# The third last batch's routed row turned on TensorE, and the tiles behind the branch in a loop

## The chip, the core and the metric

The kernel runs on one core of a Trainium2 chip. The metric is the device time of one execution in microseconds (us). Five engines work side by side, each with its own instructions in a fixed order: TensorE (PE, with its weight loads PEld), VectorE (DVE), ScalarE (ACT), GpSimd (POOL) and SyncE (SP). SP issues most of the DMA transfers here, POOL those with computed addresses (scatters).

## The reference, cut to what matters

Two layers work on 16 batches of 256 tokens of width 256. Each layer is a cross attention and a feed-forward part, each added to x. The last part is a mixture of eight experts, and the change touches the way into it:

```
x = x + _L0_xattn_ref(ctx_1024, layernorm(x), ...)      # 8 heads of 128
x = x + _L0_ffn_ref(layernorm(x), ...)                  # weights depend on the batch's own tokens
x = x + _L1_xattn_ref(layernorm(x), ctx_1024, ctx_1024, ...)
x = x + _L1_ffn_ref(layernorm(x), ...):
    inh     = sigmoid(x @ Wr / temperature)             # 8 numbers per token
    weights = exp(-|inh - c| / 0.1) inside a zone, else the two nearest experts; normalized
    out     = sum over e of weights[e] * ((silu(x @ Wg[e]) * (x @ Wu[e])) @ Wd[e])
```

A token whose weight for an expert is zero need not be computed by it. The kernel sorts the tokens by expert and computes only those.

## The kernel before, in words

**Batches.** A batch goes through a front part (heads: `s0q`, `s0k`, `s1`, `s2`, `s3`) and a chain (`chain(b, A, behind)`): output projection `px`, feed-forward (`ph`, gelu, `pf`), second attention (`pv`, `pq`, `sc`, `po`), then the **row**: x normalized once more, with the token's number behind it. `row` is what the experts read, and it is also multiplied by the router's weights `Wr` (product `pl`, result `z`). `route(b, A, mine)` turns z into the eight weights (VectorE lines 737 to 787), counts the tokens of each expert (`pn`), works out slots, and scatters the rows into a DRAM tensor `slots_d` by POOL, 16 indirect DMAs per batch (line 811). Batches 0 to 11 are part 0 of the experts' work, 12 to 15 part 1.

**Turning.** Matmul needs its operand with the width on the partitions, so every normalized tile is transposed. There are two ways. `to_blocks` and `from_blocks` transpose 32 x 32 blocks on VectorE, write them to DRAM and read them back in the other order (a hop: one DMA out, four back, all from SP). `turned_tile` transposes 128 x 128 on TensorE into PSUM and copies the result out on ScalarE. A flag `hopped = b < B - 2` chooses for all four places in `chain`, so batches 14 and 15 are turned on TensorE and batches 0 to 13 hop. The place of the row is lines 616 to 629.

**Order.** The order on each engine is written by the program as it builds the kernel. `chain`, `route` and `experts` are generators; a `yield` gives a time (us of PE work, kept in `Clock.pe`) before which the job is not to be taken up again, and `gap()` lets waiting jobs put their next unit behind the heads' work. So a changed `yield` moves all that comes after it. `evict` copies a PSUM result out on ScalarE, or on VectorE while ScalarE is planned to be busy with a gelu (`Clock.act_free`). PSUM tiles of the tag "mm" turn through six buffers in the order in which they are asked for.

**Experts.** `experts(lists, ...)` starts with the last heads (batch 15, head 4 on) and runs beside the chains of batches 13 to 15. A group `G` is up to four tiles of 128 tokens of one expert, named by part, expert and first tile (group 0_4 of expert 0 is its tiles 4 to 6). Per group: `load` of rows from `slots_d`; turning (`turn_rows` on TensorE for the first two groups, a hop `send_rows` / `fetch_rows` for the others); gate `pg` and up `pu` for two halves; down `pd`; the weighted result `o` added into the output by a POOL DMA (line 1324).

**The branch.** Each expert has fixed room (`CAPS`). Tokens beyond it go through single tiles `U`, whose place and expert `plan()` works out on the chip (`Plan.starts`, `Plan.who`, `Plan.weigh`). Three such tiles are always computed among the groups (`AMONG = (2, 1)`); more would run behind `tc.If(some > 0)`, and if those do not suffice, `V` tiles in loops run over all slots.

Of the kernel before, what the change touches and what calls it, by code (L numbers as in the profile page):

```python
# [12 lines left out]
F32 = mybir.dt.float32  # L13
# [3 lines left out]
ALU = mybir.AluOpType  # L17
AX = mybir.AxisListType

P = 128  # L20
# [9 lines left out]
def xattn_ffn_kernel(  # L30
# [10 lines left out]
    nc = tc.nc  # L41
    B, S, D = x.shape
# [4 lines left out]
    E = Wg.shape[0]  # L47
# [39 lines left out]
    class Job:  # L87
# [3 lines left out]
        def __init__(self, units):  # L91
            self.units, self.ready, self.done = units, 0.0, False
# [12 lines left out]
    def apart(ins, group, others=()):  # L105

        for g in (group, *others):
            tc.declare_no_dep(
                ins.ins, group=g, reason="rows of one group go to different places"
            )  # L110
        tc.add_to_no_dep_group(group, ins.ins)
        nc.gpsimd.nop()
# [52 lines left out]
    UNITS = (6, 1)  # L165

    AMONG = (2, 1)
# [89 lines left out]
    ROW = D + E + 1  # L257
# [42 lines left out]
    def to_blocks(pool, src, C, tag, bufs, name, most=None):  # L300
        tb = pool.tile(
            [P, C * D], F32, tag=tag, bufs=bufs, name=name, padded_shape=[P, most or C * D]
        )
        tb = tb.rearrange("p (m d c s) -> p m d c s", m=QP, d=DC, c=C)
        for c in range(C):
            nc.vector.transpose(
                tb.rearrange("p m d c s -> p d m c s")[:, :, :, c, :],
                src[:, c, 0:D].rearrange("p (d m r) -> p d m r", d=DC, m=QP),
            )
        hop = dram.tile([P, QP, DC * C * QB], F32, tag=f"{tag}{C}", name=f"hop_{name}")  # L310
        nc.sync.dma_start(hop, tb.rearrange("p m d c s -> p m (d c s)"))
        return hop

    def from_blocks(dst, hop):
        from_ = hop.rearrange("(a r) m f -> m r a f", r=QB)
        for m in range(QP):
            nc.sync.dma_start(dst[ts(m, QB)].rearrange("r a d c s -> r a (d c s)"), from_[m])  # L317

    def in_order(t):

        return t.rearrange("p a d c s -> p d c a s")
# [25 lines left out]
    def chain(b, A, behind):  # L347
# [12 lines left out]
        hopped = b < B - 2  # L360
# [3 lines left out]
        def raw_tile(tag, name):  # L364
            return wk.tile([P, QP, DC, TC, QB], F32, tag=tag, name=name)

        def turned_tile(src, tag, name):
            t = wk.tile([P, DC, S], F32, tag=tag, bufs=1, name=name)
            nc.scalar.copy(t, transposed(src, f"{name}_p"))
            return t  # L370
# [24 lines left out]
        y = wk.tile([P, TC, D], F32, tag="y", name=f"yb_{b}")  # L395
# [22 lines left out]
        if hopped:  # L418
# [3 lines left out]
            yT, latents = in_order(yTb), yTb[:, 0, :, 0, :]  # L422
            there = Clock.pe + LANDED
        else:
            yield 2.2
            yT = latents = turned_tile(y, "yT", f"ybT_{b}")
# [99 lines left out]
        y = wk.tile([P, TC, D], F32, tag="y", name=f"yc_{b}")  # L526
# [86 lines left out]
        row = A.row[b] = wk.tile([P, TC, ROW], F32, tag="row", bufs=2, name=f"row_{b}")  # L613
        ln_apply(row[:, :, 0:D], x_b, mv, rs)
        nc.vector.tensor_copy(row[:, :, D + E], number[:, b * TC : (b + 1) * TC])
        if hopped:
            hop = to_blocks(wk, row, TC, "tbc", 2, f"yd_{b}_b")
            yield SENT
            raw = raw_tile("raw_c", f"ydT_{b}")
            from_blocks(raw, hop)  # L620
            yield LANDED
            ydT = wk.tile([P, DC, S], F32, tag="q1T", name=f"ydT_{b}")
            for d in range(DC):
                evict(ydT[:, d, :], in_order(raw)[:, d], None, None)
            yield 4.0
        else:
            yield 1.4
            ydT = turned_tile(row, "q1T", f"ydT_{b}")
            yield 1.6
# [201 lines left out]
    with ExitStack() as sh, ExitStack() as sa, ExitStack() as sf:  # L831
# [82 lines left out]
        def evict(out, src, bias, scale):  # L914

            if Clock.pe >= Clock.act_free:
                if bias is None:
                    nc.scalar.copy(out, src)  # L918
                else:
                    nc.scalar.activation(out, src, AF.Identity, bias=bias, scale=scale)  # L920
            elif bias is None:
                nc.vector.tensor_copy(out, src)
            else:
                nc.vector.tensor_scalar(out, src, scale, bias, ALU.mult, ALU.add)
# [259 lines left out]
        def add_chain(b, behind):  # L1184
            job = Job(chain(b, A, behind))
            A.tails[b] = Job(route(b, A, job))
            line.extend([job, A.tails[b]])
            return job
# [34 lines left out]
        class G:  # L1223
# [7 lines left out]
            def load(self):  # L1231
                self.rows = D_.front.tile(
                    [P, self.tiles, ROW], F32, tag="rows", name=f"rows_{self.name}",
                    padded_shape=[P, TG, ROW],
                )
                nc.sync.dma_start(
                    self.rows,
                    slots_d[self.part][self.first : self.first + self.tiles * P, :].rearrange(
                        "(t p) f -> p t f", p=P
                    ),  # L1240
                )
# [98 lines left out]
        def others(part):  # L1340

            k = 1 - part
            return [f"out_{k}_{e}" for e in range(E)] + [f"out_{k}_u{j}" for j in range(UNITS[k])]

        class U:


            def __init__(self, part, j):
                self.part, self.j = part, j
                self.u = sum(UNITS[:part]) + j  # L1350
                self.name = f"{part}_u{j}"

            def place(self):
                return nc.values_load(
                    Plan.starts[0:1, self.u : self.u + 1], engines=(mybir.EngineType.SP,),
                    min_val=0, max_val=E * NTOKS[self.part] - P,
                )

            def expert(self):
                return nc.values_load(  # L1360
                    Plan.who[0:1, self.u : self.u + 1], engines=(mybir.EngineType.PE,),
                    min_val=0, max_val=E - 1,
                )

            def weight(self, to):
                by = D_.more.tile([P, E], F32, tag="by_u", bufs=2, name=f"by_{self.name}")
                nc.vector.tensor_tensor(by, self.rows[:, D : D + E], Plan.weigh[:, self.u], ALU.mult)
                nc.vector.tensor_reduce(to, by, AX.X, ALU.add)

            def load(self):  # L1370
                tag = ("y", "yT")[self.u % 2]
                rows = wk.tile(
                    [P, ROW], F32, tag=tag, bufs=1, name=f"rows_{self.name}",
                    padded_shape=[P, DC * S],
                )
                self.rows = rows
                nc.sync.dma_start(rows, slots_d[self.part][bass.ds(self.place(), P), :])
# [37 lines left out]
            def down(self):  # L1415
# [13 lines left out]
                )  # L1429
                apart(ins, f"out_{self.name}", others(self.part))  # L1430

        class V(U):


            def __init__(self, part, e, t, j):
                self.part, self.u = part, j
                self.e, self.t = e, t
                self.name = f"{part}_v{j}"

# [107 lines left out]
        for n in range(NS + 2):  # L1547
            b, h = divmod(n, H)
# [55 lines left out]
        some = nc.values_load(beyond[0:1, 0:1], min_val=0, max_val=1)  # L1604
        all_slots = nc.values_load(beyond[0:1, 1:2], min_val=0, max_val=1)
        with tc.If(some > 0):
            for part in range(2):
                for j in range(AMONG[part], UNITS[part]):
                    u = U(part, j)
                    u.load()  # L1610
                    u.turn()
                    u.gates()
                    u.turn_h()
                    u.down()

            with tc.If(all_slots > 0):
                for part in range(2):
                    with tc.For_i(0, E) as e:
                        with tc.For_i(0, (NTOKS[part] - CAPS[part]) // P, 2) as t:
                            pair = [V(part, e, t + j, j) for j in range(2)]  # L1620
                            for v in pair:
                                v.load()
                            for v in pair:
                                v.turn()
                                v.gates()
                                v.turn_h()
                                v.down()
# [38 lines left out]
```

## Time and profile before

| what | value |
|---|---|
| median of three runs | 1810.41 us (1808.53 to 1811.94) |
| the profiled execution's own time | 1815.16 us |
| its span, first to last instruction | 1813.4 us |
| mean granted TensorE clock | 0.995 |
| HBM read and written | 161.91 MB and 161.48 MB, 178 GB/s over the span |
| last matmul group, last output DMA of POOL | 1799.8 us, 1802.6 us |

How to read it: times in the trace are microseconds from the span's start. The page gives busy shares of each engine, and the chain of work that ended last, followed back from the last instruction: an engine that is not on it costs nothing by being busy. The timeline prints start, duration, engine, line, what is written and read, and in brackets how long the engine was idle before it and which event ended that. Nearly all matmuls have line 80 (transposes line 84), the place of a helper; they are told apart by the names of their tiles. A row with xN is N instructions merged. The granted clock is the share of full speed that TensorE was given in a stretch.

The heads' part of the kernel ends at about 1460 us; from about 1430 to 1800 us the experts run.

### The profile page before, as it was taken

To read this page: it belongs to the slowest core of one execution; us is meant where nothing else is said; L and a number is where in the kernel's file an instruction comes from. 1 tells how busy PE (TensorE), PEld (TensorE's weight loads), DVE (VectorE), ACT (ScalarE), POOL (GpSimd) and SP (SyncE) were. 2 spreads that over 40 slices of the span, in tenths; PEclk is the share of its full clock that TensorE was granted. 3 is DMA by queue.
4 is the path that set the end of the run, shared out by engine and by line. 5 is a ranking of instruction groups with operands and counts; after the bars stand their busy time and mean duration, and the time that the engine had idled before them with its cause. 6 is when DMAs were issued, how large, how long until landed. Compare 5 with 4: busy or idle time off the path is not lost.

```text
span 1813.4 us, 22509 instructions
## 1 busy us (share of the span) xinstructions
PE 1780.6 (98%) x6508; PEld 1206.7 (67%) x6508; DVE 1196.6 (66%) x3332; ACT 586.0 (32%) x1306; POOL 830.9 (46%) x979
## 2 busy tenths in 40 slices
PE   8999999999999999999999999999999999999987
PEld 4566666666666666666666666666666677666655
DVE  4465676767676767676767676767666667675544
ACT  3433434343434343333333333333333311211100
POOL 2122224444435353535353535353534357776765
PEclk9999999999999999999999999999999999999999
DMA  6653546565655555555556555555545668899986
GB/s 215 184 185 117 174 139 190 167 189 168 187 169 188 168 184 172 184 172 178 173 181 174 180 177 177 179 178 175 181 156 157 197 161 216 227 234 235 200 168 112
DMA packets 264746, 325.01 MB, mean 179 GB/s; under 512 B 32893, under 2 KB 217385, under 8 KB 264617
## 3 DMA queue, kind: packets, MB, share of 16 engines
q1 hardware_dynamic: 235720, 273.67, 49.9%
q0 software_dynamic: 28848, 49.83, 11.7%
q8 instruction: 54, 0.88, 0.2%
q14 instruction: 76, 0.61, 0.1%
q10 hardware_dynamic: 48, 0.01, 0.0%
HBM read 161.91 MB, written 161.48 MB: 178 GB/s over the span
## 4 chain that ended last, share of the span: by engine, by line
PE 92%; DMA 2%; DVE 2%; SPq 1%; issue 1%; POOL 1%; ACT 0%; POOLq 0%; DVEq 0%; ACTq 0%
PE po L80 13%; PE sc L80 13%; PE pv L80 13%; PE pk L80 11%; PE pq L80 7%; PE px L80 6%; PE ph L80 6%; PE pf L80 6%; PE pg L80 5%; PE pu L80 5%; PE pd L80 5%; DMA yTd<-hop_rows_b 1%; PE pl L80 1%; SPq L317 1%; DMA pT<-hop 0%
## 5 line engine op out<-in xcount | busy, mean ns | idle before, releaser
L987 ACT ACTIVATE pr<-sc,nm 128x512 f32<-128x512 f32 x256 | 173.7, 683 | 479.7 <-DVE nm L981 418.4
L995 POOL TENSOR_SCALAR pr<-pr,ri 128x512 f32<-128x512 f32 x256 | 179.0, 709 | 322.7 <-DVE ri L994 317.8
L811 POOL DMA_INDIRECT slots_d<-row,at_slot x256 | 253.2, 989 | 70.4 <-issue 70.4
L80 PE MATMUL po<-pT,v 128*128 128x256 f32 x1024 | 242.3, 379 | 2.6 <-DVE W2T L1048 1.5
L80 PE MATMUL sc<-kT,qT 128*128 128x512 f32 x512 | 241.0, 593 | 1.5 <-ACT kT L920 1.5
L80 PE MATMUL pk<-kvT,Wk_sb 128*128 128x512 f32 x512 | 241.3, 594 | 0.0
L80 PEld LDWEIGHTS po<-pT,v 128*128 128x128 f32 x1024 | 193.8, 190 | 70.8 <-issue 38.1
L80 PE MATMUL pv<-Wv_sb,kvT 128*128 128x512 f32 x512 | 235.0, 592 | 0.0
L1033 DVE TENSOR_SCALAR outT<-po,cvec 128x256 f32<-128x256 f32 x128 | 61.2, 478 | 246.0 <-PE po L80 230.1
L1003 DVE STREAM_TRANSPOSE tb<-pr 128x512 f32<-128x512 f32 x256 | 165.9, 686 | 13.2 <-DMA hop<-tb 11.7
L80 PEld LDWEIGHTS pv<-Wv_sb,kvT 128*128 128x128 f32 x512 | 97.0, 190 | 108.2 <-issue 103.1
L981 DVE TENSOR_REDUCE nm<-sc 128x1 f32<-128x512 f32 x256 | 160.3, 663 | 2.0 <-PE sc L80 1.9
L80 PEld LDWEIGHTS sc<-kT,qT 128*128 128x128 f32 x512 | 96.9, 190 | 69.9 <-issue 61.2
L80 PEld LDWEIGHTS pk<-kvT,Wk_sb 128*128 128x128 f32 x512 | 97.7, 191 | 68.4 <-issue 61.6
L80 PE MATMUL pq<-kvT,Wq_sb 128*128 128x256 f32 x512 | 133.5, 383 | 0.0
L80 PEld LDWEIGHTS pq<-kvT,Wq_sb 128*128 128x128 f32 x512 | 96.7, 191 | 41.8 <-issue 28.2
L80 PE MATMUL px<-Wo_sb,outT 128*128 128x256 f32 x512 | 121.8, 381 | 0.0
L80 PE MATMUL ph<-ybT,W1e 128*128 128x256 f32 x512 | 121.0, 379 | 0.0
L1324 POOL DMA_INDIRECT out_dram<-o,at x65 | 102.3, 1574 | 36.3 <-issue 19.2
L452 POOL TENSOR_TENSOR W2e<-ev,od 128x256 f32<-128x256 f32 x120 | 78.5, 681 | 88.0 <-DMA ev<-ev_d 88.0
L918 ACT COPY v<-pv 128x512 f32<-128x512 f32 (+1 forms) x132 | 70.8, 536 | 148.1 <-PE pv L80 146.7
L80 PE MATMUL pf<-W2e,hT 128*128 128x256 f32 x512 | 118.0, 379 | 0.0
(259 smaller groups left out, 2695.4 us busy)
## 6 DMA issues: line engine op xcount, KB each, us to landing
hop<-tb SPq DMA_DIRECT2D x128, 512.0 KB
pT<-hop SPq DMA_DIRECT2D x512, 128.0 KB
ev<-ev_d SPq DMA_DIRECT2D x32, 512.0 KB
rows<-slots_d SPq DMA_DIRECT2D x14, 530.0 KB
hop_rows_b<-rows_b SPq DMA_DIRECT2D x13, 512.0 KB
yTd<-hop_rows_b SPq DMA_DIRECT2D x52, 128.0 KB
rows<-slots_d SPq DMA_DIRECT2D x15, 397.5 KB
hop_rows_b<-rows_b SPq DMA_DIRECT2D x14, 384.0 KB
```

What stands on the lines that cost most here:

```text
L80: nc.tensor.matmul(out, lhsT, rhs, **kw)
L317: nc.sync.dma_start(dst[ts(m, QB)].rearrange("r a d c s -> r a (d c s)"), from_[m])
L452: (nc.gpsimd if b < B - 1 else nc.vector).tensor_tensor(W2e[:, c, d, :].rearrange("p (i a) -> p i a", i=NI), evs[1][:, :, c * NA : (c + 1) ...
L811: ins = nc.gpsimd.indirect_dma_start(out=slots_d[part], out_offset=bass.IndirectOffsetOnAxis(ap=at_slot[:, c, e : e + 1], axis=0), in_=row ...
L918: nc.scalar.copy(out, src)
L981: nc.vector.tensor_reduce(nm, sc, AX.X, ALU.max, negate=True)
L987: nc.scalar.activation(pr, sc, AF.Exp, bias=nm, accum_out=sm)
L995: nc.gpsimd.tensor_scalar(pr, pr, ri, 1.0, ALU.mult, ALU.mult)
L1003: nc.vector.transpose(tb[:, :, c, :], heads[n][c][0].rearrange("p (m f) -> p m f", m=QP))
L1033: nc.vector.tensor_scalar(o, po, col("bv", h), None, ALU.add)
L1324: ins = nc.gpsimd.indirect_dma_start(out=out_rows[0 : sum(NTOKS[: self.part + 1]), :], out_offset=bass.IndirectOffsetOnAxis(ap=self.at[:, ...
```

## The change

Two edits. The row of batch 13, the third last, is turned on TensorE: the condition at the row's place is `b < B - 3` instead of `hopped`. All else of batch 13 still hops. With it the `yield` values of that place change for batch 13, from 6.5, 7.5 and 4.0 to 1.4 and 1.6.

And the four extra tiles of part 0 behind the branch, written out one after the other before, become one body in a loop with the tile's number in a register (`class W`). Part 1 had none there.

```diff
-        if hopped:
+        if b < B - 3:
             hop = to_blocks(wk, row, TC, "tbc", 2, f"yd_{b}_b")
             yield SENT
             raw = raw_tile("raw_c", f"ydT_{b}")
...
-                self.u = sum(UNITS[:part]) + j
+                u = self.u = sum(UNITS[:part]) + j
+                self.of = slice(u, u + 1)
+                self.tag = ("y", "yT")[u % 2]
...
-                    Plan.starts[0:1, self.u : self.u + 1], engines=(mybir.EngineType.SP,),
+                    Plan.starts[0:1, self.of], engines=(mybir.EngineType.SP,),
...
-                    Plan.who[0:1, self.u : self.u + 1], engines=(mybir.EngineType.PE,),
+                    Plan.who[0:1, self.of], engines=(mybir.EngineType.PE,),
...
-                nc.vector.tensor_tensor(by, self.rows[:, D : D + E], Plan.weigh[:, self.u], ALU.mult)
+                nc.vector.tensor_tensor(
+                    by, self.rows[:, D : D + E],
+                    Plan.weigh[:, self.of].rearrange("p u e -> p (u e)"), ALU.mult,
+                )
...
+        class W(U):
+            def __init__(self, j):
+                self.part, self.u = 0, j
+                self.name = "0_w"
+                self.of = bass.ds(j, 1)
+            tag = "y"
...
-            for part in range(2):
-                for j in range(AMONG[part], UNITS[part]):
-                    u = U(part, j)
-                    u.load()
-                    u.turn()
-                    u.gates()
-                    u.turn_h()
-                    u.down()
+            with tc.For_i(AMONG[0], UNITS[0]) as j:
+                u = W(j)
+                u.load()
+                u.turn()
+                u.gates()
+                u.turn_h()
+                u.down()
```

`class V` gets its tag from j as before, by another line.

## The prediction

> **What bounds the kernel.** I read the page first: which engine is full, and what its idle time waits for.
>
> ```profile
> PE 1780.6 (98%) x6508; PEld 1206.7 (67%) x6508; DVE 1196.6 (66%) x3332; ACT 586.0 (32%) x1306; POOL 830.9 (46%) x979
> ```
>
> TensorE (PE) is busy in 98% of the span and is 92% of the chain that ended last. So the change counts only through PE work added or removed and PE waits opened or closed. I next asked for PE's waits from 1400 us on, the only part where the order changes:
>
> ```profile
> PE pg L80 <- DMA yTd<-hop_rows_b: 5.9, 4, 2.8
> PE pl L80 <- ACT ydT L918: 1.9, 1, 1.9
> PE ycT_p L84 <- DVE yc L282: 0.8, 1, 0.8
> ```
>
> The second is the one wait that the changed hop causes; the columns are total, times, longest. The timeline around it shows both the cause and an after-effect:
>
> ```profile
> 1424.82 0.76 DVE L306 STREAM_TRANSPOSE yd_b<-row 128x256 f32<-128x256 f32 x2
> 1425.98 0.38 SPq L311 DMA_DIRECT2D hop_yd_b<-yd_b  x1
> 1432.48 2.90 SPq L317 DMA_DIRECT2D ydT<-hop_yd_b  x4
> 1437.02 0.71 ACT L918 COPY ydT<-ydT 128x256 f32<-128x256 f32 x2 [5.93 <-DMA ydT<-hop_yd_b]
> 1437.48 1.14 PE L80 MATMUL pl<-Wr_sb,ydT 128*128 128x8 f32 x8 [1.94 <-ACT ydT L918]
> 1438.84 2.94 PE L80 MATMUL pg<-yTd,wx 128*128 128x512 f32 x4
> 1441.57 2.56 PE L80 MATMUL pu<-yTd,wx 128*128 128x512 f32 x4
> ```
>
> The row is transposed at 1424.8 and back at 1437.0; PE idles 1.94 us before the router product pl. Then pg and pu (1.72 us a group in the chain where nothing disturbs them) take 2.77 and 2.36 in the chain. That is the granted clock, 0.93 in the stretch 1440 to 1460 against 1.00 beside it: 1.05 + 0.64 = 1.69 us more.
>
> **Removed.** (1) The pl wait and its after-effect: 1.94 + 1.69 = 3.63 us of PE. (2) Two VectorE transposes (0.76), five DMA issues of SP (0.38 + 2.90), two ScalarE copies (0.71): none on PE's path after pl, worth nothing by themselves. (3) Today pg of group 0_4 comes right behind its own turn, at 1452.93, and takes 1.64 instead of 1.29: 0.35 us. It moves away from there; what it meets is below. Sum 3.98.
>
> **Added in front.** Four TensorE transposes now stand between pk (its successor po started at 1424.17) and po. Batch 14's, at 1571.61, delay the next matmul by 0.50 us. They need the row, which VectorE writes till 1424.84:
>
> ```profile
> 1423.40 1.44 DVE L282 TENSOR_SCALAR row<-x,mv_d,rs_d 128x256 f32<-128x256 f32 x2
> ```
>
> The first 128 tokens are there at about 1424.1, the second at 1424.84. So PE waits 0.6 to 0.7 us in the middle, and po starts at about 1425.30: 1.13 us added. Queued behind that wait are po, pl, sc and all of PE. The ScalarE copy (0.59) lies under po (1.72). pl itself (0.8) only moves.
>
> **The moved step.** The order listing of the new kernel shows more than the diff: with pl 12 us earlier, the router's vector chain (L737 to L787) moves from after 1448 to straight behind head 7, ahead of the work that feeds PE, and pg of group 0_4 is emitted before the pf products, right behind the turn it needs, whose second half VectorE now evicts (ScalarE did). VectorE is in order, so I walk it, start to start, from today's rows.
>
> - pl ends at 1427.85, z at 1428.3 (pl to z took 0.99 at batch 15). Behind z stand head 6's transposes (1.22) and nm of head 7 (1.25): to 1430.8. Mask (0.35), two hT (1.0), reciprocals, at, wt: 1432.3. ScalarE has the exponentials by 1432.6; its table load at L735 (1.28) moves behind the gelu, under sc of batch 14.
> - Router chain: 1.1 + 1.6 (L743 to L769), outT 0.45, 1.57 (L778 to L787): 1437.4.
> - A W2e add beside POOL's products (1.0, as the row below has it), head 7's transposes 1.22, an add 0.65, sg 0.79, hTd 0.60, an add 0.60, at and wt 0.14, the eviction of half one 0.46: 1442.8. Transposes of rows_0_7 1.01, an add 0.65, sg 0.79, hTd 0.65, half two 0.55: 1446.5.
>
> ```profile
> 1432.73 1.08 DVE L460 TENSOR_TENSOR W2e<-W2e,W2T 128x512 f32<-128x512 f32 x1
> 1440.97 0.55 DVE L922 COPY yTd<-rowsT 128x384 f32<-128x384 f32 x1
> 1441.43 1.09 DVE L306 STREAM_TRANSPOSE rows_b<-rows 128x256 f32<-128x256 f32 x3
> ```
>
> PE meanwhile: po to 1427.0, pl 1427.85, sc 1429.6, ph 1431.3, eight turns 1432.3, po 1434.0, pg and pu 1437.45, three turns 1437.8, pg and pu 1441.3, three turns 1441.65. Now pg of 0_4: its first half waits to 1442.8 (1.15), runs 0.65, its second waits from 1443.45 to 1446.55 (3.1). PE sum 4.25, and all of PE is queued behind it. Bounds: if VectorE has no backlog the eviction follows its turn by the 0.35 us of today; if everything slips by the 1.1 us of three contended adds, 5.4. I take 4.25, since each duration has its own row.
>
> What such a gap does to the clock is in the tail:
>
> ```profile
> 1743.12 3.57 PE L80 MATMUL pg<-yTd,wx_all 128*128 128x512 f32 x4 [2.79 <-DMA yTd<-hop_rows_b]
> 1760.60 3.54 PE L80 MATMUL pg<-yTd,wx_all 128*128 128x512 f32 x4 [2.58 <-DMA yTd<-hop_rows_b]
> ```
>
> A wait of 2.79 us is followed by a pg of 3.57 instead of 1.72: 1.85 us. The Trainium skill (TensorE: Matmul & The Clock Gate, HAM oscillation) says that gaps over about 3.4 us are what has to be avoided. By that rule today's 1.94 us has no after-effect and neither has my 3.1: removed 2.29, added front and waits 5.38. By the rows: removed 3.98, added 5.38 + 1.85. The rows decide (gaps of 1.94, 2.58 and 2.79 all paid): 1.85.
>
> One more: pd of group 0_0 needs the PSUM buffer of pg 0_4, freed by sg, which on VectorE now stands behind the statistics of both pf: about 0.6.
>
> Net in this stretch: 1.13 + 4.25 + 1.85 + 0.6 - 3.98 = **+3.85 us**.
>
> **Downstream.** POOL runs gapless from 1474 to 1511 with batch 13's 16 scatters (about 1.3 us each) among the outputs; they move into its idle time of 1437 to 1475, where it waits 16.98 and 9.35 us. So rs_q of batch 15 comes earlier, and PE now has pg and pu (2.6 us) ahead of ycT_p: I credit its 0.8. The last scatter of batch 15 moves two outputs back in POOL's order (+3.7), but POOL reaches group 3_0 some 3 to 5 us sooner; with PE 3 us later, the two waits at 1676 and 1677.75 (0.40, 0.32) should about halve: 0.4. The tail's 2.79 and 2.58 are hop times after small groups and stay.
>
> **The loop behind the branch.** Only tiles beyond the planned ones run there; the trace has three rows_u loads, all planned, so the body is jumped over before and after. It gets shorter. No row prices such a jump; after the last output at 1804.1 only 9.3 us of landing and end are left. I take 0, bounds -1 and +1.
>
> **Sum.** 3.85 - 0.8 - 0.4 = +2.65, say +2.6. The profiled execution took 1815.16 (span 1813.4 and 1.8 around it): 1817.8. The runs' median, 1810.41, lies 4.75 below it, so the forecast is **1813.0 us**. A measurement of this kernel tells apart some 0.2%, 3.6 us, so this counts as no change, near the edge.
>
> **Rivals.** *The stall does not come* (VectorE gets through in time, since the W2e adds or the router chain overlap more than their starts show): 4.25 + 1.85 + 0.6 shrink to 0.35, so 1.13 + 0.35 - 3.98 - 1.2 = -3.7, and with POOL's lead also shortening a tail hop, -4.5: 1806. For it: VectorE is 66% busy and today ends that stretch idle. Against: today it idles there because ScalarE, not VectorE, was late. *The stall is longer* (slower): one mechanism, VectorE's backlog ahead of half two. Each us beyond 1446.5 is a us of PE; from 1447.5 the total passes +3.6. With three adds at 1.08 and the gap of 1.15 also long enough to cost half a clock window (0.9), and no downstream credit: +3.85 + 1.1 + 0.9 = +5.9, 1816.3. For it: L460 took 1.08 and 1.01 beside POOL. *The change hides itself*: PE's gain and the new wait cancel, within 1 us: 1810.4; for it, both are of one size.
>
> **Chances.** Forecast 0.45 (own range 1810 to 1816; a third of it above +3.6). No stall 0.24. Longer stall 0.23. Cancelled 0.08. Faster by over 0.2%: 0.19, from the second. Slower: 0.21 + 0.15 = 0.36. Within: 0.45. The range reaches both rivals with their bounds: 1805.5 to 1818.5.
>
> **What would show it.** After: no DMA into ydT before 1440; pl at about 1427; ydT_p waits about 0.6 for row; a PE wait of over 2.5 us at pg on an eviction (L922) at about 1443 to 1447, with a pg or pf at half speed behind it; batch 13's scatters before 1485. If the L922 wait is under 1 us, my VectorE walk is wrong and the kernel is faster; if PE waits elsewhere between 1450 and 1640 for over 1 us, the downstream part is.

## The result and the profile after

| kernel | median | against the kernel before, beside it |
|---|---|---|
| before | 1810.24 us (18 runs) | |
| after | 1814.43 us (1811.95 to 1817.52, 18 runs) | 1.0023, 95% interval 1.0016 to 1.0030 |

The change costs 4.2 us, just over what a measurement of this kernel tells from nothing. The profiled execution took 1817.5 us (span 1815.8, granted clock 0.994). The page's first line, engine busy times, hardly moved:

```profile
PE 1782.5 (98%) x6512; PEld 1208.1 (67%) x6513; DVE 1195.6 (66%) x3331; ACT 585.3 (32%) x1304; POOL 830.5 (46%) x979
```

Four matmuls more are the four turns. As before, only waits can tell. PE's waits from 1400 us on (total, times, longest):

```profile
PE pg L80 <- DVE yTd L922: 5.5, 2, 3.0
PE pg L80 <- DMA yTd<-hop_rows_b: 3.6, 2, 2.7
PE hT_u L84 <- DVE h_u L1412: 3.2, 1, 3.2
PE ydT_p L84 <- DVE row L282: 0.4, 1, 0.4
```

The waits for the hop at pl and for yc are gone, as meant. In their place TensorE waits 5.5 us for two copies of VectorE. The timeline of the changed kernel shows where (start, duration, engine, line, output and input, and in brackets the idle time before it):

```profile
1423.97 0.55 PE L84 MATMUL ydT_p<-ident,row 128*128 128x128 f32 x3 [0.37 <-DVE row L282]
1426.08 0.95 PE L80 MATMUL pl<-Wr_sb,ydT 128*128 128x8 f32 x8
...
1431.36 0.62 DVE L743 TENSOR_TENSOR wt<-wt,mask 128x16 f32<-128x16 f32 x1
...
1438.47 0.17 DVE L787 TENSOR_SCALAR rest<-wt 128x16 f32<-128x16 f32 x1
...
1440.22 0.49 PE L84 MATMUL rowsT<-ident,rows 128*128 128x128 f32 x3
...
1442.32 0.69 DVE L460 TENSOR_TENSOR W2e<-W2e,W2T 128x512 f32<-128x512 f32 x1
...
1443.07 0.55 DVE L922 COPY yTd<-rowsT 128x384 f32<-128x384 f32 x1
1443.67 0.91 PE L80 MATMUL pg<-yTd,wx 128*128 128x384 f32 x2 [2.96 <-DVE yTd L922]
1444.54 0.65 DVE L460 TENSOR_TENSOR W2e<-W2e,W2T 128x512 f32<-128x512 f32 x1
1445.11 0.68 DVE L1309 SCALAR_TENSOR_TENSOR sg<-sg,pg 128x512 f32<-128x512 f32 x1
...
1445.90 0.69 DVE L1310 TENSOR_TENSOR hTd<-sg,pu 128x512 f32<-128x512 f32 x1
1446.50 0.55 DVE L922 COPY yTd<-rowsT 128x384 f32<-128x384 f32 x1
1447.11 1.65 PE L80 MATMUL pg<-yTd,wx 128*128 128x384 f32 x2 [2.52 <-DVE yTd L922]
1448.55 3.36 PE L80 MATMUL pf<-W2e,hT 128*128 128x256 f32 x8
```

Read it from the turn: `rowsT`, the second half of group 0_4, is done at 1440.7, and its copy starts at 1446.50. VectorE had the routing chain (L743 to L787) from 1431.4 to 1438.6, and from there to 1446.5 it was busy with work that stands in front of the copy. Behind the second wait pg takes 1.65 us, against 0.91 for its first half, and pf 3.36, against 1.89 in the trace of before. The stretch in five pieces of 3.41 us (length, PE busy and number of matmuls, granted clock, DMA share, GB/s), TensorE alone:

```profile
1437.87:1441.28 3.41, 2.84 (x9) 1.00 0.00 0
1441.28:1444.69 3.41, 0.91 (x2) 1.00 0.49 190
1444.69:1448.11 3.42, 1.00 (x2) 0.50 0.96 285
1448.11:1451.52 3.41, 3.41 (x9) 0.50 0.83 233
1451.52:1454.93 3.41, 3.41 (x19) 1.00 0.69 222
```

Two of them ran at half clock (slow pieces, as they are called from here on): 0.50 + 1.71 = 2.2 us lost. So the stretch fits the forecast's story. The total does too, but the experiments show that it hides two errors of opposite sign.

### The profile page after: what moved, and what is told of

Same layout as the page of the kernel before. It is cut to its first block, busy times and chain, and to the rows that moved or that the text cites. A ratio compares the mean times of both kernels' runs of the same rounds, so it can differ in the third digit from the quotient of the medians.

```text
span 1815.8 us, 22495 instructions
## 1 busy us (share of the span) xinstructions
PE 1782.5 (98%) x6512; PEld 1208.1 (67%) x6513; DVE 1195.6 (66%) x3331; ACT 585.3 (32%) x1304; POOL 830.5 (46%) x979
```

## The experiments

The theory at the start: all of the 4.2 us comes from the stretch between 1424 and 1461 us, where VectorE's backlog holds TensorE. Rivals: the turning on TensorE itself costs; the loop behind the branch costs; the tail costs. "The loop alone" and "the row alone" below are the two edits taken singly.

| run | median, us | ratio, 95% interval |
|---|---|---|
| e1 row alone | 1815.25 | 1.0030 (1.0018 to 1.0041) |
| e2 loop alone | 1805.71 | 0.9980 (0.9971 to 0.9989) |
| e3 second eviction on ScalarE | 1809.62 | 1.0001 (0.9992 to 1.0010) |
| e4 both evictions on ScalarE | 1807.73 | 0.9987 (0.9978 to 0.9996) |
| e5 after, again | 1812.99 | 1.0016 (1.0005 to 1.0026) |
| e6 one tile behind the branch | 1806.14 | 0.9978 (0.9965 to 0.9990) |
| e7 turned on TensorE, order kept | 1805.29 | 0.9975 (0.9965 to 0.9985) |
| e8 routing chain later | 1811.68 | 1.0012 (1.0001 to 1.0022) |
| e9 routing chain later still | 1812.47 | 1.0025 (1.0016 to 1.0035) |
| e10 pg later | 1807.24 | 0.9988 (0.9977 to 1.0000) |
| e11 before, one execution | 1809.34 | |

The kernel before had medians of 1809.96 (beside e1 to e4), 1809.64 (e5 to e8) and 1808.15 us (e9 and e10). Ratios are the safer reading; 0.001 is 1.8 us.

### e1 and e2: one edit at a time

e1 is the kernel before with only

```diff
-        if hopped:
+        if b < B - 3:
```

> Only the condition on the row is changed; the tiles behind the branch stay written out. Theory (all of the +4.2 us comes from the reordered stretch at 1424 to 1461 us): the same as the changed kernel, 1814.4 us, within 1 us. Rival (the loop behind the branch, or the shorter program, costs): 1810.2 to 1812.

Measured: 1815.25 us, as slow as the whole change. e2 is the changed kernel with that line put back.

> Only the tiles behind the branch are looped; the row of batch 13 still takes the hop. Theory: the same as before, 1810.2 us, within 1 us; the bounds that the prediction gave were -1 and +1. Rival (the loop costs): 1812 to 1814.

Measured: 1805.71 us, 3.6 us (0.9971 to 0.9989) below before. Neither the theory nor the rival had this: code that never runs makes the kernel faster. The end of the trace tells how. The instructions of the line of the branch, `tc.If`, on GpSimd's queue, in the kernel before (count, shortest/median/longest in ns, first and last start):

```profile
L1606 POOLq EVENT_SEMAPHORE  x4: 17/43/4756, 1802.8 to 1807.8; - x4
...
L1606 POOLq COMPARE_BRANCH  x1: 53/53/53, 1802.3 to 1802.3; - x1
...
L1606 POOLq INC_SWDGE_SEM  x1: 1034/1034/1034, 1807.9 to 1807.9; - x1
```

The same in e2, where the line is 1620:

```profile
L1620 POOLq EVENT_SEMAPHORE  x2: 43/43/43, 1800.2 to 1800.3; - x2
...
L1620 POOLq COMPARE_BRANCH  x1: 53/53/53, 1799.7 to 1799.7; - x1
L1620 POOLq INC_SWDGE_SEM  x1: 1044/1044/1044, 1800.4 to 1800.4; - x1
```

GpSimd takes the branch at 1802.3. With four tiles written out, four steps on semaphores follow on its queue, and one of them waits 4.76 us, until some 3.6 us after the last output was issued (1804.1). Only then come the 1.03 us of INC_SWDGE_SEM and a drain of 3.5 us. With the loop there are two steps, none waits, and the drain runs while the outputs still land. The last output and the drain before, then the same in after, which has the loop (the drain is the longest of its three):

```profile
1802.60 1.54 POOL L1324 DMA_INDIRECT out_dram<-o_more,at  x1 [0.30 <-issue]
L1661 POOLq DRAIN  x3: 46/107/3543, 1808.9 to 1813.0; - x3
...
1807.75 1.55 POOL L1324 DMA_INDIRECT out_dram<-o_more,at  x1 [0.30 <-issue]
L1674 POOLq DRAIN  x3: 46/112/5879, 1809.1 to 1815.5; - x3
```

What the long step waits for stands in the traces too, which keep the semaphores of every instruction. GpSimd's last outputs use the semaphores 111 to 118 in turn. In before, the last output uses 113, which rises for the last time at 1807.70, when this output has landed; the long step waits for 117 and 113 and ends at 1807.73. In e1 the two times are 1807.78 and 1807.80, in e11 1801.96 and 1801.99. So GpSimd waits for its own last output. With the loop the steps name only 114 to 118, of outputs issued earlier. From the landing of the last output to the end of the span it takes 5.66 or 5.67 us in the three traces with four tiles written out, and 3.05 to 3.07 us in the ten others.

From the start of the last output to the end of the span it takes 10.8, 10.3 and 10.3 us where four tiles are written out (before, e1, e11), and 8.0, 7.6, 7.4, 8.1, 7.6, 7.0, 7.8, 7.5 and 7.9 us in the nine traces with the loop (after, e2 to e5, e7 to e10): 10.5 against 7.7 on average, **2.8 us** less. Of this 2.6 us lie behind the landing; the landing itself takes 3.7 to 5.1 us and differs from trace to trace. The runs of e2 say 3.6 us, with an interval of 2.0 to 5.2 that holds 2.8.

### e6: is it the loop, or the number of tiles?

The kernel before, with fewer tiles written out:

```diff
-                for j in range(AMONG[part], UNITS[part]):
+                for j in range(AMONG[part], min(UNITS[part], AMONG[part] + 1)):
```

> The kernel before, with only the first of the four tiles behind the branch written out (the other three are left out; none of them runs on these inputs). Theory (GpSimd, which jumps over the four tiles, first waits at the branch for its last outputs to land, 4.8 us, because four tiles' scatters use more of the semaphores that must be made up for): with one tile that wait is gone or short, and from the start of the last output to the end of the span it takes about 7.6 us instead of 10.8: 1806 to 1807.5 us. Rival (only the form of a loop does it, whatever the number of tiles): 1810 us and 10.8 us.

Measured: 1806.14 us, and 6.7 us from the last output's start to the end of the span. The branch on GpSimd's queue of e6 shows the wait gone:

```profile
L1606 POOLq EVENT_SEMAPHORE  x2: 42/42/43, 1797.7 to 1797.8; - x2
```

So the number of bodies counts, not the loop's form. The count of semaphores fits: one tile and the four `V` bodies behind it skip five output DMAs, and the steps of e6 name five semaphores (114 to 118), as with the loop; four tiles and the `V` bodies skip eight, and the steps of before name all eight, 113 among them. Two or three tiles written out were not tried.

### e5: the changed kernel again

> The changed kernel once more, on the chip of the runs beside it. If row and loop simply add (row alone +5.3, loop alone -4.2 us), it comes out near 1811 us; if the first measurement holds, 1814.4. The wait at the end of the run is in both cases like that of the loop alone: from the start of the last output to the end of the span 7.6 to 8 us, against 10.8 before.

Measured: 1812.99 us, between the two, 7.6 us from the last output's start to the end. Its two waits for the evictions sum to 4.8 us (e1: 5.0), and two slow pieces follow them again. Loop and row add up within their intervals: -3.6 and +5.4 us make +1.8, with some 2.6 us either way, against +2.9 and +4.2 measured. The row's cost is 5.4 us by e1, and 4.2 + 2.8 = 7.0 us by the change less the loop's trace.

### e3 and e4: take the copies off VectorE

Group 0_4's evictions are fixed to ScalarE, which idles there (9.49 us before its next operation in the trace of after). e3 moves the second half, e4 both:

```diff
-                evict(
-                    in_order(self.yT)[:, d],
...
+                if (self.part, self.e, self.first) == (0, 0, 4 * P) and d == 1:
+                    nc.scalar.copy(out, src)
+                else:
+                    evict(out, src, None, None)
```

> The changed kernel, with the second eviction of group 0_4's turned rows on ScalarE, which idles from 1439.3 to 1448.8 us. Theory (VectorE's backlog ahead of the two evictions holds TensorE): the second wait on an eviction, 2.5 us, goes, and about 1.5 us of slow clock behind it; the first, 3.0 us, stays: 1810.5 us. Rival (the four added turns and their wait for the row are what costs): no change, 1814.4. Rival (TensorE's wait only moves to the next product of the stretch): 1813 to 1814.

> The changed kernel, with both evictions of group 0_4's turned rows on ScalarE. Theory: both waits (2.96 and 2.52 us) and the slow clock behind them (about 2.3 us) go, less 0.5 us for VectorE's waits that open behind it: 1807 us, 3 us below the kernel before. Rival (the added turns cost): 1814.4, no change. Rival (the wait moves to the next product): 1812 to 1814. If the lead is eaten by the tail (scatters of batch 15, outputs on GpSimd): 1810 to 1811.

Measured: 1809.62 and 1807.73 us, as the theory had it (1810.5 and 1807), and not as any rival had it. In e3 one wait on L922 of 3.0 us is left, in e4 none; pg of 0_4 then waits 1.05 us for VectorE's `sg` (most likely for the PSUM buffer that this frees). The copies are most of the answer; e4 is still 2.0 us above e2, with intervals that overlap.

### e7: turn on TensorE, keep the order

```diff
-            yield 1.4
+            yield SENT + LANDED if b == B - 3 else 1.4
             ydT = turned_tile(row, "q1T", f"ydT_{b}")
-            yield 1.6
+            yield 4.0 if b == B - 3 else 1.6
```

> The changed kernel with the turn of batch 13's row put where the hop would have landed (14.0 instead of 1.4 before the turn, 4.0 instead of 1.6 behind it), so that the rest of the work keeps the order of before. Theory (the moved routing chain is what costs, turning on TensorE does not): no wait at pl, no wait on the evictions of group 0_4, four turns (0.5 us) added: 1805 us, at or below the loop alone (1805.7). Rival (turning on TensorE costs): 1810 or more.

Measured: 1805.29 us. The turn stands where the hop would have landed, and it costs what was said; the timeline of e7 around it:

```profile
1428.83 1.89 PE L80 MATMUL po<-pT,v 128*128 128x256 f32 x8
1430.56 0.60 PE L84 MATMUL ydT_p<-ident,row 128*128 128x128 f32 x4
1431.00 1.88 PE L80 MATMUL pg<-yTd,wx 128*128 128x512 f32 x4
...
1442.55 5.34 PE L80 MATMUL pf<-W2e,hT 128*128 128x256 f32 x24
1447.73 0.49 PE L84 MATMUL rowsT<-ident,rows 128*128 128x128 f32 x3
1448.05 1.64 PE L80 MATMUL pg<-yTd,wx 128*128 128x384 f32 x4
```

0.44 us for the turn, no wait before pl, and no bracket in the whole stretch. So **turning on TensorE does not cost; the early place that the short yields gave it does.** e7 and e2 differ by 0.4 us, less than their intervals. Both are faster than the kernel before and the kernel after.

### e8, e9 and e10: the chain, or the place of pg?

The early pl moves two things: VectorE's routing chain to the front, and pg of 0_4 to directly behind its turn. e8 and e9 hold the chain back:

```diff
         A.weighed.add(b)
-        yield 4.0
+        yield 14.0 if b == B - 3 else 4.0
```

> The changed kernel with the routing chain of batch 13 held back (14.0 instead of 4.0 behind its masks); pl stays early. Theory (VectorE's backlog): with the chain behind the work that feeds TensorE both waits on the evictions of group 0_4 shrink to under 1 us together: 1806 to 1808 us. Rival (the added turns and the wait for the row cost): 1813 to 1814.

Measured: 1811.68 us, not 1806 to 1808. PE's waits of e8 from 1400 us on:

```profile
PE pg L80 <- DVE yTd L922: 4.1, 1, 4.1
```

The first wait is gone, but twelve operations of the chain (some 2.7 us) still stand in front of the second copy, and two slow pieces come with the longer wait, from 1443.6 us on. e9 has 24.0 in place of 14.0, which puts all of them behind it.

> The changed kernel with the whole routing chain of batch 13 behind the second eviction of group 0_4 (24.0 instead of 4.0 behind its masks); pg of 0_4 stays directly behind its turn. Worked out from the trace of e8: there the second half waited 4.07 us, of which 2.75 us of VectorE were the chain's twelve operations. Theory A (chain and place of pg share the blame): the wait shrinks to about 1.3 us and costs no or one slow clock window: 1807 to 1809 us. Theory B (the chain is all of it): no wait, 1805.5. Theory C (only the place of pg counts): the wait stays near 4, 1811.

Measured: 1812.47 us, which none of its theories had. PE's waits of e9 from 1400 us on:

```profile
PE ycT_p L84 <- DVE yc L282: 3.7, 1, 3.7
PE pg L80 <- DVE yTd L922: 1.8, 1, 1.8
```

The wait for the copy did shrink, to 1.8 us (1.3 expected). But the chain now holds up the normalized row of batch 14, and TensorE waits 3.7 us for that, with one slow piece from 1462.2 us on. VectorE has this work to do somewhere; holding it back only moves the bill. e10 leaves chain, turn and copies as in the changed kernel and holds pg back, so that pf and po stand between the turn and pg again:

```diff
+                if n == 1:
+                    yield 9.0
                 for i in range(IC):
                     g.gate(i)
```

> The changed kernel with pg of group 0_4 held back by 9.0 so that the products pf and po stand between its turn and it, as before the change; turn, pl and routing chain stay early, and both evictions stay on VectorE. Theory A (place of pg): the pf products, 7 us, cover VectorE's backlog, no wait on L922, no slow window: 1805 to 1806.5 us. Theory B (the chain holds up other work that TensorE needs as well): a wait of 1 us or more at pf or pu, 1808 to 1811.

Measured: 1807.24 us, between its theories, nearer to A. PE's waits of e10 from 1400 us on:

```profile
PE pf L80 <- DVE sg L1309: 1.1, 1, 1.1
PE pf L80 <- DVE W2e L460: 0.7, 1, 0.7
```

No wait on L922 is left and no slow piece follows, while 1.7 us of waits on other work of VectorE remain. So the row's cost splits thus: after to e10, 1.0023 and 1.0016 to 0.9988, some 5 to 6 us, is pg directly behind its turn while VectorE has the early chain (e4 gets nearly as much back by moving the copies); e10 to e7, 0.9988 to 0.9975, about 2 us with overlapping intervals, is the early chain; its waits in e10 are shown, its price is less sure.

### e11: the kernel before, a second trace

> The kernel before once more, for a second trace. Its first profiled execution took 1815.2 us, 4.8 above the median, with three slow clock windows of 3.4 us each. If the windows depend on where the gaps fall in a fixed grid of 3.41 us, the same waits (1 to 2 us at pl, 2 to 3 us twice at pg near 1743 and 1760 us) need not cost the same windows here: two or fewer would be followed by one in an execution of about 1810; three would speak for waits that always cost.

Measured: 1809.34 us, two slow pieces before the end of the matmuls, at 1739.3 and 1756.4, and none behind pl. The timeline of e11:

```profile
1434.57 1.14 PE L80 MATMUL pl<-Wr_sb,ydT 128*128 128x8 f32 x8 [1.12 <-ACT ydT L918]
1435.57 0.53 PE L84 MATMUL rowsT<-ident,rows 128*128 128x128 f32 x3
1435.93 1.88 PE L80 MATMUL pg<-yTd,wx 128*128 128x512 f32 x4
```

The hop's wait is 1.12 us here, not 1.94, and pg behind it runs at full speed (1.88). The trace on which the forecast was built showed the dear case.

## Why the prediction was right, and where it was not

The forecast was 1813.0 us, measured 1814.43. The sign was right, the range held, and the likeliest case (a small loss by VectorE's backlog) came true. Step by step:

- **Removed, the hop's wait and its after-effect (3.63): too large.** In the four traces with a hop the wait is 1.94, 1.06, 1.1 and 1.12 us (before, e2, e6, e11), and a slow piece follows in the first two only. At about 1.7 us a slow piece the mean is 1.3 + 0.85, some 2.2 us. About 1.5 us were credited that a usual execution doesn't have. Taking the profiled execution's 4.75 us off the end result did not mend this, as it left the removed term at its size.
- **Added in front (1.13): 1.1 us** (po starts 2.81 us behind pk in after, 1.72 in before), 0.37 of it a wait. Right.
- **VectorE's walk (4.25): 5.5, 4.8 and 5.0 us** (after, e5, e1). Place and cause right, the sum a little small. It was split otherwise: the first wait is 2.96 instead of 1.15 us, the second 2.52 instead of 3.1. The chain took 7.3 us where the walk has 4.8, as it now runs beside POOL's products (below), and the W2e adds behind it (L460), one of which the walk had put beside POOL, were clear of POOL.
- **After-effect (1.85): two slow pieces, 2.2 us.** Right in kind.
- **PSUM buffer at pd (0.6): did not come**; such waits came in e4 and e10 instead.
- **Downstream (-0.8 and -0.4): the first came, but smaller** (no wait for yc in after; the wait of before is 0.8 us in its first trace and 0.3 in e2, e6 and e11), **the second is open.** The waits of the tail differ by as much between two executions of one program: `hT_u` waits 3.2 us in the first trace of after and 0.8 in e5.
- **The loop (0, bounds -1 and +1): wrong. It gives 2.8 us**, and this is the step that failed. The prediction looked at "the jump" and "9.3 us of landing and end" and took the latter as fixed. The row that would have shown it stood in the trace of before: a step of 4.76 us at the line of the branch, on the queue of the engine that ends last. It is not counted as busy time, so no list of costly groups has it.

So the row was put at +2.65 and costs 5.4 to 7.0; the loop was put at 0 and gives 2.8. With the sizes above, the row's terms sum to 1.1 + 5.1 + 2.2 - 2.2 - 0.35 - 0.3, some 5.6 us, near e1's 5.4 (an estimate; the 0.35 us of pg's old place was not measured again). That the total came near is luck: the two misses have opposite signs. Of the rivals, "the stall is longer" had the row's mechanism and its size (+5.9). "The stall doesn't come" failed on the two waits at L922, and "the change hides itself" describes the sum but not by its mechanism.

## What to carry to other kernels

When a step becomes faster in a kernel whose order is set by planned times, its place may move more than its cost: e7 took the faster turn and left the place, and some 8 us lie between it and the change. A product directly behind its own turn has no cover for the copy in between, and a busy VectorE makes it pay. Look at the queues of every engine at a branch that isn't taken: written-out bodies behind it can make the engine that ends last wait, though nothing in them runs; here the skipped DMAs were enough for their turn of semaphores to reach the one of the last output.

## What the hardware showed that was not expected

**Slow clock comes in a fixed grid.** In each trace all stretches at half clock start at whole multiples of 3.413 us from one another. The record of the clock in the first trace of before:

```
slow from (us)    length    steps of 3.413 us since the one before
1439.53           3.41
1743.31           3.41      89.0
1760.38           3.41       5.0
1804.75          10.72      13.0   (matmuls have ended)
```

The offset of this grid differs from execution to execution. What counts is how much of one grid window TensorE idles. In the 13 traces, at full clock and from 20 us on, windows with 2.0 us or more of idle were followed by a slow one, those with 1.8 or less were not; between lie 1.90 (followed) and 1.94 (not followed). Two windows with less idle were followed too, 1.37 and 1.06 us (before, e2); both hold pl, whose matmuls have only eight columns. But the window of e11 that holds most of pl had 1.12 us of idle and was not followed, so what made the difference there is not shown. In windows already slow, 0.8 us was enough for a second. So a gap that falls across a border can be free. In e3 the wait of 2.97 us fell 1.69 and 1.28 us into two windows (length, busy of PE, PEld, DVE, ACT, POOL, granted clock, DMA share, GB/s):

```profile
1437.29:1440.71 3.42, 1.73 (x7) 0.72 (x5) 3.32 (x7) 0.80 (x2) 0.00 (x0) 1.00 0.32 132
1440.71:1444.12 3.41, 2.13 (x8) 1.52 (x9) 3.40 (x10) 0.49 (x1) 0.00 (x0) 1.00 0.49 145
1444.12:1447.53 3.41, 3.41 (x20) 3.05 (x19) 1.33 (x5) 0.00 (x0) 0.00 (x0) 1.00 0.98 293
```

The clock stays at 1.00, where shorter waits of 1.94 and 1.06 us cost a slow window elsewhere. The Trainium skill (TensorE: Matmul & The Clock Gate, Part 1: The HAM clock gate) says that the window of 3413 ns runs freely; these traces agree. The length of a gap, by which both the rule about 3.4 us and the rows were weighed in the prediction, is not the measure. A part of the spread between runs goes with the clock: of the kernel before beside e1 to e4 (1806.8 to 1813.8 us), the runs at a mean granted clock of 0.995 took 1811.5 us on average (5 runs), at 0.996 1810.2 (16) and at 0.997 1809.0 (6). That the place of the grid decides a run's clock is likely, but was not tested by itself.

**VectorE's small operations slow down beside POOL's products.** One line of the routing chain in after, at 1432.7 us, while POOL computes W2e (the tile `same`; shortest/median/longest in ns):

```profile
L753 DVE TENSOR_TENSOR same<-dist x1: 699/699/699, 1432.7 to 1432.7; 128x128 f32<-128x128 f32 x1
```

The same in e8, at 1437.6, with POOL idle:

```profile
L753 DVE TENSOR_TENSOR same<-dist x1: 283/283/283, 1437.6 to 1437.6; 128x128 f32<-128x128 f32 x1
```

In all 13 traces this line ran six times beside POOL's products, for 695 to 699 ns, and 202 times clear of them, for 276 to 289 ns. The five operations of two SBUF inputs from L743 to L762 take 3.14 us in after and 1.30 us in e8. The walk of the prediction had taken their rows from a place where POOL was idle.
